# A macaron block on one core: the scheduler's durations replaced by measured ones, a slot's registers loaded once, router logits taken from the projection's product

## The chip, the core and the metric

The kernel runs on one core of a Trainium2 chip. The metric is device time in microseconds (us) of one launch. The engines have short names: PE (TensorE; PEld is its loading of weights), DVE (VectorE), ACT (ScalarE), POOL (GpSimd) and SP (SyncE, which here only issues DMAs and loads the registers that they need).

## What is computed

The input is 8 sequences of 256 tokens of 128 values (2048 tokens, 16 tiles of 128), all in float32. Six steps update it in place:

```
x = x + 0.5 * moe(layernorm(x))              # layer 0
x = x + attention(layernorm(x))              # 16 heads of 8
x = x + 0.5 * moe(layernorm(x))              # layer 1, the same weights
x = x + 0.5 * channel_mix(layernorm(x))
x = x + gated_long_convolution(layernorm(x)) # FFT of 512, filter made by a small network
x = x + 0.5 * channel_mix(layernorm(x))

def moe(s):                                  # 8 experts, each token goes to 2
    h = rmsnorm(s @ W_in.T, in_norm_w)
    logits = h @ Wr.T
    idx = top_2(logits + expert_bias);  gates = softmax(logits[idx])
    out = sum over the 2 experts e of
          gates[e] * rmsnorm((silu(h @ Wg[e].T) * (h @ Wu[e].T)) @ Wd[e].T, enorm_w[e])
    return rmsnorm(out, out_norm_w) @ W_out.T
```

## The kernel before

**Dispatch.** Both expert layers go through the tokens in four groups of four tiles (`dispatch`). A group is transposed by PE (`flip`), multiplied with the input projection (`product`, L587: four matmuls of 128x128 into one PSUM bank) and with the router's weights, which are already folded behind the projection (`logits`, L591: four matmuls with 8 columns into a second bank). DVE chooses the two experts of each token (`choice`), matmuls with a triangle of ones count the tokens of each expert (`ranks`), and POOL sends every token's row twice into a table in DRAM, `hs`, sorted by expert, with eight indirect DMAs (`scatter`, L721).

**Tables and slots.** `table` turns the counts into a list of 39 slots of 128 rows. There are two tables per layer: the one after half of the tokens gives the first 9 slots (`NFULL`), whose rows are certain by then, and the one after all of them gives the other 30. A slot (`slot`) belongs to one expert. SP makes three transfers for it: the rows (`hst`, 64.5 KB, L897), the gate and up weights (`w`, 512 KB, L889) and the down weights with the norm's weight (`wd`, 320 KB, L893). The address of each depends on the table, so SP first loads a register from it: one `values_load` for each of the three transfers (L888, L892, L896). Then PE transposes the rows (L907), does four gate and four up matmuls (L920, L924) and four down matmuls (L976); ACT and DVE do the activation between them and the norm behind them, and POOL sends the result to a second table `y2` with one indirect DMA (L1000). There are 4 buffers for `w`, 4 for `wd`, 5 for `hst`. `combine` reads `y2` back and adds to x. Then come attention (`attend`, L1192 scores and L1258 averages), the second expert layer in the same way, and the channel mixes and the convolution.

**The order.** Nothing is issued in the order of the source. Every piece of work is recorded with `plan.add`: the engines that may do it, the cost in us on each, and what it reads and writes. `Plan.best` then lists all pieces in up to 20 rounds: a forward pass (`order`) places pieces by rank on the engine that is free first and hands out buffers and PSUM banks, a backward pass (`reverse`) makes new ranks from the result, and the round with the shortest planned end is kept. That order is then issued, so each engine, SP's queue too, is an in-order list fixed when the kernel is built. The costs are formulas such as

```
def mm_(n, cols):
    return n * (0.012 + 0.00175 * cols)
def dma(nbytes, run, **k):
    return plan.add({"SP": 0.08}, lambda e: run(), size=nbytes, **k)
```

and a DMA is planned to land 2 us after its bytes passed at 250 GB/s, one transfer behind the other (`FLIGHT`, `RATE`).

Of the kernel before, what the change touches and what calls it, by code (L numbers as in the profile page):

```python
# [41 lines left out]


def mm_(n, cols):
    return n * (0.012 + 0.00175 * cols)


def dve_(cols):
    return 0.15 + cols / 960


def act_(cols, more=0.0):
# [25 lines left out]
class Plan:  # L78
# [8 lines left out]
    def add(self, engines, run, r=(), w=(), p=(), lag=0.0, table=None, size=0, boost=0.0):  # L87
        o = Op()
        o.engines, o.run, o.lag, o.table, o.size, o.boost = engines, run, lag, table, size, boost
        o.n, o.after, o.bufs = len(self.ops), [], []  # L90
        for x in (*r, *w, *p):
            if isinstance(x, Buf) and x not in o.bufs:
                o.bufs.append(x)
                self.bufs[x] = self.bufs.get(x, 0) + 1
        wait = set()
        for x, sides in [(x, (0, 1)) for x in r] + [(x, (0, 1, 2)) for x in w] + [(x, (0, 2)) for x in p]:
            s = self.state.setdefault(x, ([], [], []))
            for side in sides:
                wait.update(s[side])
        for x in r:  # L100
            self.state[x][2].append(o)
        for x in w:
            self.state[x] = ([o], [], [])
        for x in p:
            self.state[x][1].append(o)
        o.wait = wait
        o.flight = lag + (self.FLIGHT + size / self.RATE if size else 0.0)
        for b in wait:
            b.after.append(o)
        self.ops.append(o)  # L110
        return o
# [164 lines left out]
    "k4": ([P, 1024], 7),  # L276
    "k2": ([P, 516], 12),
    "k1": ([P, 256], 6),
    "hst": ([P, ROW], 5),
    "yrow": ([P, ROW], 3),  # L280
    "d": ([P, D], 5),
# [6 lines left out]
def macaron_kernel(ctx: ExitStack, tc: tile.TileContext, a: dict, out: bass.AP):  # L288
# [18 lines left out]
        return plan.add({"POOL": cost}, lambda e: run(), **k)  # L307

    def pe(cost, run, **k):
        return plan.add({"PE": cost}, lambda e: run(), **k)  # L310

    def dma(nbytes, run, **k):
        return plan.add({"SP": 0.08}, lambda e: run(), size=nbytes, **k)

    def bc_last(ap, n):
        return ap.unsqueeze(len(ap.shape)).to_broadcast([*ap.shape, n])
# [1 line left out]
    def sm():  # L318
        return Buf("sm")
# [18 lines left out]
    def X(t, n=1):  # L338
        return [("x", i) for i in range(t, t + n)]
# [157 lines left out]
    def normed_t(n, t0, wide=False):  # L497

        st = spread(n, t0)
        mr = sm()  # L500

        def scales():
            s = st.v(3 * n, "p (k t) -> p k t", k=3)
            nc.vector.tensor_scalar(mr.v(n), s[:, 0], 1.0 / D, LN_EPS, ALU.mult, ALU.add)
            nc.vector.tensor_scalar(s[:, 1], s[:, 1], 0.5, None, ALU.mult)

        dve(2 * TINY, scales, r=[], w=[st, mr])
        power(mr, n)
# [12 lines left out]
        for i in range(n):  # L521
            plan.add(
                {"POOL": 0.79, "DVE": 0.28},
                lambda e, i=i: one(e, i),
                r=[st, mr, *X(t0 + i)],
                p=[xn],
            )
        pt = Buf("bank")
        pe(0.1 * n, lambda: flip(lambda t: xn.ap[:, ts(t, D)], n, pt), r=[xn, "ident"], w=[pt])
# [19 lines left out]
        return xt  # L549
# [20 lines left out]
    def dispatch(f, t0, n, half):  # L570
        L = layer[f]
        tag = f"{f}_{t0}"
        pt, ph, pl, xt = Buf("bank"), Buf("bank"), Buf("bank"), Buf("k2")
        pe(0.1 * n, lambda: flip(lambda t: xs[:, t0 + t, :], n, pt), r=["ident", *X(t0, n)], w=[pt])
        act(act_(n * P), lambda: nc.scalar.copy(xt.v(n * P), pt.v(n * P)), r=[pt], w=[xt])
        st = spread(n, t0)
        z = sm()
# [4 lines left out]
            w=[z],  # L582
        )

        def product():
            for t in range(n):
                nc.tensor.matmul(ph.ap[:, ts(t, D)], xt.ap[:, ts(t, P)], win_r[:, 0:D], start=True, stop=True)  # L587

        def logits():
            for t in range(n):  # L590
                nc.tensor.matmul(pl.ap[:, ts(t, E)], xt.ap[:, ts(t, P)], win_r[:, D : D + E], start=True, stop=True)  # L591

        h, ll = Buf("k2"), sm()
        pe(mm_(n, D), product, r=[xt, "win_r"], w=[ph])
        pe(n * 0.07, logits, r=[xt, "win_r"], w=[pl])
        plan.add(
            {"ACT": act_(n * D), "DVE": dve_(n * D)},
            lambda e: nc.scalar.copy(h.v(n * D), ph.v(n * D))
            if e == "ACT"
            else nc.vector.tensor_copy(h.v(n * D), ph.v(n * D)),  # L600
            r=[ph],
            w=[h],
        )
        dve(TINY, lambda: nc.vector.tensor_copy(ll.v(n * E), pl.v(n * E)), r=[pl], w=[ll])
        sq, ss = Buf("k2"), sm()

        def square(t):
# [76 lines left out]
                r, ident, before.unsqueeze(1).to_broadcast([P, n + 1, E]), start=False, stop=True  # L684
            )

        pe(0.07 * (n + 2), ranks, r=[mask, "tri", "ones", "ident", prev], w=[pr])

        def place():
            v = nc.vector  # L690
# [188 lines left out]
    def slot(f, t, silu):  # L879
# [4 lines left out]
        hst, w, wd = Buf("hst"), Buf("w"), Buf("wd")  # L884
        need = [("hs", f, 0)] if early else [("hs", f, 0), ("hs", f, 1)]

        def weights():
            e = nc.values_load(tab[t : t + 1, 1:2], engines=[SP], min_val=0, max_val=E - 1)  # L888
            nc.sync.dma_start(w.ap, a["wall"][bass.ds(e, 1), :, 0 : 2 * DFF].rearrange("o p f -> p (o f)"))  # L889

        def weights_down():
            e = nc.values_load(tab[t : t + 1, 1:2], engines=[SP], min_val=0, max_val=E - 1)  # L892
            nc.sync.dma_start(wd.ap, a["wall"][bass.ds(e, 1), :, 2 * DFF : WALL].rearrange("o p f -> p (o f)"))  # L893

        def rows():
            row = nc.values_load(tab[t : t + 1, 0:1], engines=[SP], min_val=1, max_val=HS_ROWS - P)  # L896
            ins = nc.sync.dma_start(hst.ap, L["hs"][bass.ds(row, P), :])  # L897
            if early:
                alone(ins, [f"hsr{f}_0"], [f"hs{f}_1"])
                for name in L["sent"]:  # L900
                    tc.add_manual_dep(ins.ins, name, behind_data, reason="rows of the first half")

        dma(P * ROW * 4, rows, r=[("tab", f, stage), *need], w=[hst])
        dma(P * 2 * DFF * 4, weights, r=[("tab", f, stage)], w=[w])
        dma(P * (DFF + D) * 4, weights_down, r=[("tab", f, stage)], w=[wd])
        pt, ht = Buf("bank"), Buf("d")
        pe(0.12, lambda: nc.tensor.transpose(pt.v(P), hst.ap[:, 0:D], ident), r=[hst, "ident"], w=[pt])  # L907
# [7 lines left out]
        )  # L915
        pair, sg, hg = Buf("pair"), Buf("k2"), Buf("k2")

        def gate():
            for k in range(NFC):
                nc.tensor.matmul(pair.ap[:, 0, ts(k, P)], w.ap[:, ts(k, P)], ht.ap, start=True, stop=True)  # L920

        def up():
            for k in range(NFC):
                nc.tensor.matmul(  # L924
                    pair.ap[:, 1, ts(k, P)], w.ap[:, DFF + k * P : DFF + k * P + P], ht.ap, start=True, stop=True
                )

        pe(mm_(4, P), gate, r=[w, ht], p=[pair], w=[("g", f, t)])
        pe(mm_(4, P), up, r=[w, ht], p=[pair], w=[("u", f, t)])
        if silu:  # L930
            act(
                act_(DFF),
# [91 lines left out]
    def combine(f, t0, n, half):  # L1024
# [61 lines left out]
        pe(0.1 * n, lambda: flip(lambda t: acc.ap[:, ts(t, D)], n, pt), r=[acc, "ident"], w=[pt])  # L1086
# [82 lines left out]
    def attend(seqs, lead):  # L1169
# [24 lines left out]
        def set_(parts):  # L1194
# [10 lines left out]
                    pair.v2 = pair.ap.rearrange("p j (i k) -> p j i k", i=2)  # L1205
                product(parts)

            pe(mm_(2, S), run, r=r, w=w)

        def top(s, js, pair):  # L1210
            m = ms[s % NM][:, :, js[0] : js[0] + 2, HD].rearrange("p i j -> p j i")
# [7 lines left out]
        def turn_top(s):  # L1219
# [10 lines left out]
            pe(0.2, run, r=[("m", s % NM), ("m", s % NM, 0), ("m", s % NM, 2), "ident"], w=[pt])  # L1230
# [50 lines left out]
        def finish(b):  # L1281
            o = osb[b]
            cc, ct = Buf("k1"), Buf("k1")
            for i in range(2):
# [13 lines left out]
                pe(0.4, turn, r=[o, "ident"], w=[pt])  # L1298
                dve(0.5, scale, r=[pt], w=[rc], p=[cc])
            pc, pp = Buf("bank"), Buf("bank")  # L1300
            pe(0.2, lambda: flip(lambda i: cc.ap[:, ts(i, P)], 2, pc), r=[cc, "ident"], w=[pc])
            act(act_(S), lambda: nc.scalar.copy(ct.ap, pc.v(S)), r=[pc], w=[ct])

            def out_heads():
# [386 lines left out]
    with tc.manual_schedule(engines=None):  # L1691
        for o, e, takes, _, _ in todo:
            for b in takes:
                if b.kind in WIDE:
                    i = place[b][0]
                    b.ap = banks[:, i : i + 2] if b.kind == "pair" else banks[:, i]
                    continue
                shape, _ = KINDS[b.kind]
                b.ap = work.tile(shape, F32, tag=f"{b.kind}{place[b]}", name=f"{b.kind}_{o.n}")
            o.run(e)  # L1700

# [98 lines left out]
```

## Time and profile before

| | us |
|---|---|
| median of 6 runs | 678.08 |
| lowest and highest | 673.17 and 683.37 |
| the profiled execution, its own time | 679.43 |
| its span, first to last instruction | 677.7 |
| busy: PE, weight loads, DVE, ACT, POOL | 553.7, 463.1, 372.3, 258.0, 241.8 |
| mean granted clock of PE | 0.911 |
| bytes moved by DMA | 95.41 MB, 141 GB/s over the span |

The page gives busy time of each engine, then the span in 40 slices of about 17 us, where a digit is the busy share in tenths. SP's instructions are not counted as busy: they are seen in the timeline and in the views of single source lines. "q" behind an engine's name is its sequencer. In the chain that ended last, "issue" is time in which the engine waited for nothing that the profile shows. By the trace, layer 0's slots are transposed between 62 and 241 us (the last fifteen beside attention), layer 1's first nine between 374 and 448 us and its other thirty between 464 and 568 us.

### The profile page before, as it was taken

The page shows a single profiled execution, that of the slowest core. Times are in us where ns is not written, and L with a number is a line of the kernel's source. Part 1 is how long each engine was busy: PE and PEld are TensorE (multiplying, and loading weights), DVE is VectorE, ACT ScalarE, POOL GpSimd, SP SyncE. Part 2 cuts the span into 40 slices and gives each one's busy share as a digit, 9 for nine tenths or more (in the row PEclk, how much of TensorE's full clock was granted, in tenths as well). Part 3 has the DMA queues.
Part 4 walks back from the last instruction along what each step waited for, and adds up shares of the span by engine and source line. Part 5 has one row for each costly group of instructions (what it writes and reads, how often), then busy time and mean ns, then how long its engine had stood idle before and what let it go on. Part 6 is the DMA issues. An engine that isn't in the chain of part 4 may idle for free.

```text
span 677.7 us, 14362 instructions
## 1 busy us (share of the span) xinstructions
PE 553.7 (82%) x4609; PEld 463.1 (68%) x4609; DVE 372.3 (55%) x1252; ACT 258.0 (38%) x664; POOL 241.8 (36%) x407
## 2 busy tenths in 40 slices
PE   7514888888867999888988998757888887699996
PEld 7513778888756776655655667756788886578885
DVE  4635344335846668776775864642332334778762
ACT  4421233234613546744643572312222333443022
POOL 2674755223631122343040005541332325654320
PEclk9555899899979999899996999776998999599999
DMA  5147688878766603012011513557788886200002
GB/s 131 39 117 218 188 238 279 265 230 244 253 161 182 192 17 80 1 41 65 24 56 37 194 32 114 164 193 235 240 288 278 267 256 184 63 1 1 0 1 62
DMA packets 61386, 95.41 MB, mean 141 GB/s; under 512 B 9659, under 2 KB 38498, under 8 KB 61312
## 3 DMA queue, kind: packets, MB, share of 16 engines
q1 hardware_dynamic: 56480, 84.98, 41.6%
q0 software_dynamic: 4832, 9.53, 4.0%
q8 instruction: 36, 0.59, 0.4%
q14 instruction: 38, 0.31, 0.2%
HBM read 81.68 MB, written 13.71 MB: 141 GB/s over the span
## 4 chain that ended last, share of the span: by engine, by line
PE 60%; DMA 9%; issue 9%; DVE 9%; SPq 6%; ACT 3%; POOL 2%; another core or an unknown queue 2%; DVEq 0%; ACTq 0%; POOLq 0%
PE banks L920 9%; PE banks L1192 8%; PE banks L976 8%; PE banks L924 8%; DMA hst<-hs 6%; PE banks L1258 5%; PE banks L495 2%; ACT k L1243 2%; PE banks L1588 2%; PE banks L1623 2%; PE banks L1353 2%; PE banks L1363 2%; PE banks L907 2%; DVE m L1214 1%
## 5 line engine op out<-in xcount | busy, mean ns | idle before, releaser
L1000 POOL DMA_INDIRECT y<-yrow,hst x78 | 76.8, 985 | 195.9 <-DVE yrow L993 142.7
L976 PE MATMUL banks<-wd,k 128*128 128x128 f32 x624 | 90.0, 290 | 23.1 <-DMA wd<-in_wall_dram 10.7
L488 POOL TENSOR_TENSOR sm<-sm,mhalf 128x4 f32<-128x4 f32 (+2 forms) x52 | 50.9, 985 | 152.2 <-DVE sm L615 77.6
L976 PEld LDWEIGHTS banks<-wd,k 128*128 128x128 f32 x624 | 79.8, 200 | 30.0 <-issue 9.1
L920 PE MATMUL banks<-d,w 128*128 128x128 f32 x624 | 90.8, 292 | 11.7 <-ACT d L910 4.5
L920 PEld LDWEIGHTS banks<-d,w 128*128 128x128 f32 x624 | 81.8, 205 | 17.4 <-ACT d L910 7.1
L1214 DVE TENSOR_REDUCE m<-banks 128x4 f32<-128x1024 f32 x64 | 77.5, 1222 | 27.5 <-PE banks L1192 23.0
L924 PE MATMUL banks<-d,w 128*128 128x128 f32 x624 | 89.2, 289 | 3.6 <-issue 3.3
L924 PEld LDWEIGHTS banks<-d,w 128*128 128x128 f32 x624 | 82.2, 205 | 5.5 <-issue 5.4
L1243 ACT ACTIVATE k<-banks 128x1024 f32<-128x1024 f32 x64 | 64.3, 1023 | 48.8 <-PE banks L1192 43.5
L721 POOL DMA_INDIRECT hs<-row,sm x64 | 62.1, 970 | 36.2 <-issue 24.8
L1192 PE MATMUL banks<-k,q 32*128 32x256 f32 x512 | 72.6, 420 | 1.6 <-issue 1.5
L941 DVE TENSOR_TENSOR k<-banks,k 128x512 f32<-128x512 f32 x53 | 36.6, 691 | 65.7 <-PE banks L924 35.0
L1192 PE MATMUL banks<-k,k 32*128 32x256 f32 x512 | 69.3, 409 | 1.6 <-DVE m L1214 1.0
L933 ACT ACTIVATE k<-banks 128x512 f32<-128x512 f32 x53 | 31.5, 597 | 79.0 <-PE banks L920 50.1
L1192 PEld LDWEIGHTS banks<-k,q 32*128 32x128 f32 x512 | 45.8, 197 | 15.1 <-issue 9.1
L987 ACT ACTIVATE d<-banks 128x128 f32<-128x128 f32 x78 | 21.5, 276 | 79.7 <-PE banks L976 63.4
L1192 PEld LDWEIGHTS banks<-k,k 32*128 32x128 f32 x512 | 45.6, 193 | 5.7 <-issue 1.8
L993 DVE TENSOR_TENSOR yrow<-banks,wd 128x128 f32<-128x128 f32 x78 | 22.2, 288 | 39.9 <-ACT d L987 31.2
L1258 PE MATMUL banks<-k,v 128*32 128x256 f32 x512 | 35.4, 395 | 7.7 <-ACT k L1243 4.1
L907 PE MATMUL banks<-ident,hst 128*128 128x128 f32 x78 | 22.7, 310 | 19.6 <-DMA hst<-hs 17.7
L912 DVE TENSOR_SCALAR d<-banks,inw 128x128 f32<-128x128 f32 x44 | 14.8, 348 | 33.9 <-PE banks L907 31.7
(229 smaller groups left out, 901.3 us busy)
## 6 DMA issues: line engine op xcount, KB each, us to landing
w<-in_wall_dram SPq DMA_DIRECT2D x78, 512.0 KB
wd<-in_wall_dram SPq DMA_DIRECT2D x78, 320.0 KB
hst<-hs SPq DMA_DIRECT2D x78, 64.5 KB
row<-y SPq DMA_DIRECT2D x16, 129.0 KB
row<-y SPq DMA_DIRECT2D x8, 258.0 KB
y<-yrow,hst POOLq DMA_INDIRECT x78
xs<-in_x_dram SPq DMA_DIRECT2D x4, 256.0 KB
hs<-row,sm POOLq DMA_INDIRECT x64
```

What stands on the lines that cost most here:

```text
L488: lambda: nc.gpsimd.tensor_tensor(buf.v(n), buf.v(n), mhalf.to_broadcast([P, n]), ALU.pow),
L721: ins = nc.gpsimd.indirect_dma_start(out=L["hs"], out_offset=bass.IndirectOffsetOnAxis(ap=posi.ap[:, 2 * n + 2 * t + k : 2 * n + 2 * t + k ...
L907: pe(0.12, lambda: nc.tensor.transpose(pt.v(P), hst.ap[:, 0:D], ident), r=[hst, "ident"], w=[pt])
L920: nc.tensor.matmul(pair.ap[:, 0, ts(k, P)], w.ap[:, ts(k, P)], ht.ap, start=True, stop=True)
L924: nc.tensor.matmul(pair.ap[:, 1, ts(k, P)], w.ap[:, DFF + k * P : DFF + k * P + P], ht.ap, start=True, stop=True)
L941: lambda: nc.vector.tensor_mul(hg.v(DFF), pair.ap[:, 1], sg.v(DFF)),
L976: nc.tensor.matmul(py.v(D), hg.ap[:, ts(k, P)], wd.ap[:, ts(k, D)], start=(k == 0), stop=(k == NFC - 1),)
L1000: ins = nc.gpsimd.indirect_dma_start(out=L["y2"], out_offset=bass.IndirectOffsetOnAxis(ap=hst.ap[:, D : D + 1].bitcast(I32), axis=0), in_= ...
L1192: nc.tensor.matmul(o, l, m, start=True, stop=True)
L1214: lambda: nc.vector.tensor_reduce(m, pair.v2, AX.X, ALU.max, negate=True),
L1243: lambda: nc.scalar.activation(es.v(1024, "p (j i k) -> p j i k", j=2, i=2), pair.v2, AF.Exp, scale=SCALE),
L1258: nc.tensor.matmul(po.ap[32 * j : 32 * j + 32, 0:S], vs[b % NQ][:, i, 4 * g + j, :], ess[s, j // 2 * 2].v(1024, "p (j i k) -> p j i k", j= ...
```

## The change

Three things are changed. Numbers of lines in this section's text are those of the kernel before.

1. The planner's costs are new. A group of matmuls costs 0.07 us and at least 0.224 us each, a group of transposes 0.1 us and 0.11 us each (`turn_`), DVE work 0.01 us more, and what PE makes is ready 0.12 us after its end. A DMA takes 0.42 us of SP instead of 0.08. The pieces that a piece waits for are sorted, so that the plan is the same in every build. Every piece can so get another place, another engine and another buffer.
2. A slot loads its row and its expert number into registers of SP in one piece, `registers`, planned at 0.55 us, and the three transfers use these. At most ten slots hold registers at a time. The gate and up matmuls of a slot become one piece of eight matmuls.
3. The router's logits are eight more columns of the projection's product: four matmuls of 136 columns, two in each bank of a pair, in place of four of 128 and four of 8. What copies the product and the logits out reads the pair.

```diff
 def mm_(n, cols):
-    return n * (0.012 + 0.00175 * cols)
+    return 0.07 + n * max(0.224, 0.00176 * cols)
+
+
+def turn_(n):
+    return 0.1 + 0.11 * n
 
 
 def dve_(cols):
-    return 0.15 + cols / 960
+    return 0.16 + cols / 960
...
+        wait = sorted(wait, key=lambda b: b.n)
         o.wait = wait
...
     "k1": ([P, 256], 6),
+    "regs": (None, 10),
...
     def pe(cost, run, **k):
-        return plan.add({"PE": cost}, lambda e: run(), **k)
-
-    def dma(nbytes, run, **k):
-        return plan.add({"SP": 0.08}, lambda e: run(), size=nbytes, **k)
+        return plan.add({"PE": cost}, lambda e: run(), lag=0.12, **k)
+
+    def dma(nbytes, run, issue=0.42, **k):
+        return plan.add({"SP": issue}, lambda e: run(), size=nbytes, **k)
...
-        pt, ph, pl, xt = Buf("bank"), Buf("bank"), Buf("bank"), Buf("k2")
-        pe(0.1 * n, lambda: flip(lambda t: xs[:, t0 + t, :], n, pt), r=["ident", *X(t0, n)], w=[pt])
+        pt, ph, xt = Buf("bank"), Buf("pair"), Buf("k2")
+        pe(turn_(n), lambda: flip(lambda t: xs[:, t0 + t, :], n, pt), r=["ident", *X(t0, n)], w=[pt])
...
         def product():
             for t in range(n):
-                nc.tensor.matmul(ph.ap[:, ts(t, D)], xt.ap[:, ts(t, P)], win_r[:, 0:D], start=True, stop=True)
-
-        def logits():
-            for t in range(n):
-                nc.tensor.matmul(pl.ap[:, ts(t, E)], xt.ap[:, ts(t, P)], win_r[:, D : D + E], start=True, stop=True)
...
+                nc.tensor.matmul(parts()[:, t // m, t % m, :], xt.ap[:, ts(t, P)], win_r, start=True, stop=True)
+
+        pe(mm_(n, wide), product, r=[xt, "win_r"], w=[ph])
...
-        pe(0.07 * (n + 2), ranks, r=[mask, "tri", "ones", "ident", prev], w=[pr])
+        pe(mm_(n + 2, 1), ranks, r=[mask, "tri", "ones", "ident", prev], w=[pr])
...
-        def weights():
-            e = nc.values_load(tab[t : t + 1, 1:2], engines=[SP], min_val=0, max_val=E - 1)
-            nc.sync.dma_start(w.ap, a["wall"][bass.ds(e, 1), :, 0 : 2 * DFF].rearrange("o p f -> p (o f)"))
...
+        values = {}
+
+        def registers():
+            _, (row, e) = nc.values_load_multi_w_load_instructions(
+                tab[t : t + 1, 0:2], engines=[SP], min_val=0, max_val=HS_ROWS - P
+            )
+            values["row"], values["e"] = row, nc.s_assert_within(e, 0, E - 1)
 
         def rows():
-            row = nc.values_load(tab[t : t + 1, 0:1], engines=[SP], min_val=1, max_val=HS_ROWS - P)
-            ins = nc.sync.dma_start(hst.ap, L["hs"][bass.ds(row, P), :])
+            ins = nc.sync.dma_start(hst.ap, L["hs"][bass.ds(values["row"], P), :])
...
-        dma(P * ROW * 4, rows, r=[("tab", f, stage), *need], w=[hst])
-        dma(P * 2 * DFF * 4, weights, r=[("tab", f, stage)], w=[w])
-        dma(P * (DFF + D) * 4, weights_down, r=[("tab", f, stage)], w=[wd])
+        def part(to, lo, hi):
+            nc.sync.dma_start(to.ap, a["wall"][bass.ds(values["e"], 1), :, lo:hi].rearrange("o p f -> p (o f)"))
+
+        regs = Buf("regs")
+        plan.add({"SP": 0.55}, lambda e: registers(), r=[("tab", f, stage)], w=[regs])
+        dma(P * ROW * 4, rows, r=[regs, *need], w=[hst])
+        dma(P * 2 * DFF * 4, lambda: part(w, 0, 2 * DFF), r=[regs], w=[w])
+        dma(P * (DFF + D) * 4, lambda: part(wd, 2 * DFF, WALL), r=[regs], w=[wd])
...
-        pe(mm_(4, P), gate, r=[w, ht], p=[pair], w=[("g", f, t)])
-        pe(mm_(4, P), up, r=[w, ht], p=[pair], w=[("u", f, t)])
+        pe(mm_(8, P), gate_up, r=[w, ht], p=[pair], w=[("g", f, t), ("u", f, t)])
...
-            pe(mm_(2, S), run, r=r, w=w)
+            pe(mm_(2, S) + 0.1, run, r=r, w=w)
```

More of the change, by code (lines that the diff above doesn't have):

```diff
@@ L528, in normed_t @@
         pt = Buf("bank")
-        pe(0.1 * n, lambda: flip(lambda t: xn.ap[:, ts(t, D)], n, pt), r=[xn, "ident"], w=[pt])
+        pe(turn_(n), lambda: flip(lambda t: xn.ap[:, ts(t, D)], n, pt), r=[xn, "ident"], w=[pt])
         xt = Buf("k2")
@@ L583, in dispatch, with parts, keep @@
         )
+        h, ll = Buf("k2"), sm()
+        m = n // 2
+        wide = D + E
+        def parts():
+            return ph.ap[:, :, 0 : m * wide].rearrange("p i (j d) -> p i j d", j=m)
         def product():
             for t in range(n):
-                nc.tensor.matmul(ph.ap[:, ts(t, D)], xt.ap[:, ts(t, P)], win_r[:, 0:D], start=True, stop=True)
-        def logits():
-            for t in range(n):
[L591 to L600, printed above, removed]
+                nc.tensor.matmul(parts()[:, t // m, t % m, :], xt.ap[:, ts(t, P)], win_r, start=True, stop=True)
+        pe(mm_(n, wide), product, r=[xt, "win_r"], w=[ph])
+        def keep(e):
+            dst = h.v(n * D, "p (i j d) -> p i j d", i=2, j=m)
+            src = parts()[:, :, :, 0:D]
+            nc.scalar.copy(dst, src) if e == "ACT" else nc.vector.tensor_copy(dst, src)
+        plan.add({"ACT": act_(n * D), "DVE": dve_(n * D)}, keep, r=[ph], w=[h])
+        dve(
+            TINY,
+            lambda: nc.vector.tensor_copy(
+                ll.v(n * E, "p (i j e) -> p i j e", i=2, j=m), parts()[:, :, :, D:wide]
+            ),
             r=[ph],
-            w=[h],
+            w=[ll],
         )
-        dve(TINY, lambda: nc.vector.tensor_copy(ll.v(n * E), pl.v(n * E)), r=[pl], w=[ll])
         sq, ss = Buf("k2"), sm()
@@ L885, in slot @@
         need = [("hs", f, 0)] if early else [("hs", f, 0), ("hs", f, 1)]
-        def weights():
[L888 to L893, printed above, removed]
+        values = {}
[4 more added lines that the diff above has]
+            values["row"], values["e"] = row, nc.s_assert_within(e, 0, E - 1)
         def rows():
-            row = nc.values_load(tab[t : t + 1, 0:1], engines=[SP], min_val=1, max_val=HS_ROWS - P)
-            ins = nc.sync.dma_start(hst.ap, L["hs"][bass.ds(row, P), :])
+            ins = nc.sync.dma_start(hst.ap, L["hs"][bass.ds(values["row"], P), :])
             if early:
@@ L901, in rows @@
                     tc.add_manual_dep(ins.ins, name, behind_data, reason="rows of the first half")
-        dma(P * ROW * 4, rows, r=[("tab", f, stage), *need], w=[hst])
-        dma(P * 2 * DFF * 4, weights, r=[("tab", f, stage)], w=[w])
-        dma(P * (DFF + D) * 4, weights_down, r=[("tab", f, stage)], w=[wd])
+        def part(to, lo, hi):
[5 more added lines that the diff above has]
+        dma(P * (DFF + D) * 4, lambda: part(wd, 2 * DFF, WALL), r=[regs], w=[wd])
         pt, ht = Buf("bank"), Buf("d")
-        pe(0.12, lambda: nc.tensor.transpose(pt.v(P), hst.ap[:, 0:D], ident), r=[hst, "ident"], w=[pt])
+        pe(turn_(1), lambda: nc.tensor.transpose(pt.v(P), hst.ap[:, 0:D], ident), r=[hst, "ident"], w=[pt])
         plan.add(
@@ L916, in slot, with gate_up @@
         pair, sg, hg = Buf("pair"), Buf("k2"), Buf("k2")
[L918 to L926, printed above, removed]
-        pe(mm_(4, P), gate, r=[w, ht], p=[pair], w=[("g", f, t)])
-        pe(mm_(4, P), up, r=[w, ht], p=[pair], w=[("u", f, t)])
+        def gate_up():
+            for half in range(2):
+                for k in range(NFC):
+                    nc.tensor.matmul(
+                        pair.ap[:, half, ts(k, P)],
+                        w.ap[:, half * DFF + k * P : half * DFF + k * P + P],
+                        ht.ap,
+                        start=True,
+                        stop=True,
+                    )
+        pe(mm_(8, P), gate_up, r=[w, ht], p=[pair], w=[("g", f, t), ("u", f, t)])
         if silu:
@@ L1085, in combine @@
         pt, at = Buf("bank"), Buf("k2")
-        pe(0.1 * n, lambda: flip(lambda t: acc.ap[:, ts(t, D)], n, pt), r=[acc, "ident"], w=[pt])
+        pe(turn_(n), lambda: flip(lambda t: acc.ap[:, ts(t, D)], n, pt), r=[acc, "ident"], w=[pt])
         act(act_(n * P), lambda: nc.scalar.copy(at.v(n * P), pt.v(n * P)), r=[pt], w=[at])
@@ L1228, in run @@
                     )
-            pe(0.2, run, r=[("m", s % NM), ("m", s % NM, 0), ("m", s % NM, 2), "ident"], w=[pt])
+            pe(turn_(2), run, r=[("m", s % NM), ("m", s % NM, 0), ("m", s % NM, 2), "ident"], w=[pt])
             dve(
@@ L1296, in scale @@
                     )
-                pe(0.4, turn, r=[o, "ident"], w=[pt])
+                pe(turn_(4), turn, r=[o, "ident"], w=[pt])
                 dve(0.5, scale, r=[pt], w=[rc], p=[cc])
             pc, pp = Buf("bank"), Buf("bank")
-            pe(0.2, lambda: flip(lambda i: cc.ap[:, ts(i, P)], 2, pc), r=[cc, "ident"], w=[pc])
+            pe(turn_(2), lambda: flip(lambda i: cc.ap[:, ts(i, P)], 2, pc), r=[cc, "ident"], w=[pc])
             act(act_(S), lambda: nc.scalar.copy(ct.ap, pc.v(S)), r=[pc], w=[ct])
@@ L1698, in macaron_kernel @@
                 shape, _ = KINDS[b.kind]
+                if shape is None:
+                    continue
                 b.ap = work.tile(shape, F32, tag=f"{b.kind}{place[b]}", name=f"{b.kind}_{o.n}")
```

## The prediction

> **What bounds the kernel now.** First I read the page: busy time and the slices.
>
> ```profile
> PE 553.7 (82%) x4609; PEld 463.1 (68%) x4609; DVE 372.3 (55%) x1252; ACT 258.0 (38%) x664; POOL 241.8 (36%) x407
> DMA  5147688878766603012011513557788886200002
> ```
>
> TensorE (PE) is the busiest engine, but 82% averages unlike stages. The DMA row has two humps: layer 0's expert slots (about 42 to 240 us) and layer 1's (425 to 570). So I took the slots by themselves: the transposes at L907, one per slot, in two stretches that hold little else (columns: length, PE busy and count, weight loads, clock, DMA share, GB/s).
>
> ```profile
> 84.00:160.00 76.00, 5.36 (x20) 2.69 (x20) 0.98 0.81 250
> 462.00:563.00 101.00, 8.05 (x28) 4.10 (x28) 0.95 0.82 256
> ```
>
> A slot takes 76/20 = 3.80 us in layer 0 and 101/28 = 3.61 us in layer 1. What should it take? PE: gate, up and down take 0.89 us each at full clock (chain of waits, first line below) and the transpose at most 0.33, so 2.8 to 3.0 us. DMA: a slot moves 512 + 320 + 64.5 KB in and 64.5 KB out, 0.984 MB; the second line (all engines; the last three numbers are clock, DMA share, GB/s) gives 274/0.87 = 315 GB/s at full share, so 3.12 us.
>
> ```profile
> 103.17 0.89 PE banks L924 x8
> 500.00:540.00 40.00, 34.64 (x269) 32.33 (x270) 12.82 (x30) 10.98 (x33) 11.63 (x24) 0.96 0.87 274
> ```
>
> Neither reaches 3.6. The SyncE (SP) queue does: its timeline in layer 0, one transfer after another.
>
> ```profile
> 94.69 0.33 SPq L889 DMA_DIRECT2D w<-in_wall_dram  x1
> 95.86 0.33 SPq L893 DMA_DIRECT2D wd<-in_wall_dram  x1
> 97.03 0.33 SPq L897 DMA_DIRECT2D hst<-hs  x1
> 98.18 0.47 SPq L889 DMA_DIRECT2D w<-in_wall_dram  x1
> 99.33 0.33 SPq L897 DMA_DIRECT2D hst<-hs  x1
> 100.52 0.33 SPq L893 DMA_DIRECT2D wd<-in_wall_dram  x1
> ```
>
> Five steps in 5.83 us: 1.166 us per transfer, 3.50 per slot, with hardly a wait between. SP is the limit of both stretches, though no busy row shows it. The views of the lines that issue say what fills 1.166 us (duration minimum/median/maximum, ns):
>
> ```profile
> L888 SPq TENSOR_LOAD <-tab x78: 77/274/711, 40.1 to 558.0; - x78
> L888 SPq FUSED_REGOPS  x78: 2/152/697, 40.6 to 558.4; - x78
> L888 SPq SEQ_ASSERT  x78: 3/18/402, 40.9 to 558.6; - x78
> L889 SPq FUSED_REGOPS  x78: 5/37/685, 40.9 to 558.6; - x78
> L889 SPq MOVE w<-in_wall_dram x78: 3/29/707, 41.5 to 558.8; - x78
> L889 SPq DMA_DIRECT2D w<-in_wall_dram x78: 11/333/694, 42.9 to 558.8; - x78
> ```
>
> The six medians sum to 0.843 us; with a semaphore instruction (median 0.017) 0.860. The remaining 0.306 over seven instructions is 0.044 us between two.
>
> **The change, part by part.** *Registers once.* The built program of the changed kernel has, per slot, one group of a load, two FUSED_REGOPS, three SEQ_ASSERTs and one register operation, and per transfer a FUSED_REGOPS, a semaphore instruction, a MOVE and the DMA. The group: 0.274 + 2 x 0.152 + 3 x 0.018 + 7 x 0.044 = 0.94 us, and the register operation itself, which no row shows: between 0.018 and 0.152; being one plain operation I take it like the assert, so 0.96. If the second FUSED_REGOPS no longer waits for the load it costs 0.037, and the group 0.84; high end 1.09. A transfer: 0.037 + 0.017 + 0.029 + 0.333 + 4 x 0.044 = 0.59. A slot: 0.96 + 3 x 0.59 = 2.73 us (2.6 to 2.9) against 3.50. Then DMA, at 3.12, is next late. A queue in order with four buffers of each weight does not run DMA at 100%: the best 6 us stretches of the windows are at 0.90 to 0.93. I take 3.30 us in layer 1 (share 0.945) and 3.45 in layer 0, where the filter's matmuls share PE and windows fall to 0.63. Ends: 3.12 (DMA always full) and today's 3.61 and 3.80 (nothing).
> Layer 1: 28 x 0.31 = 8.7 us (0 to 13.7). Layer 0: 20 x 0.35 = 7.0 us (0 to 13.6).
> Layer 0's last 15 slots run beside attention, where PE bounds, except in two holes (columns as in the second line two fences up):
>
> ```profile
> 192.00:198.00 6.00, 1.06 (x10) 0.87 (x8) 1.30 (x5) 0.87 (x4) 2.95 (x6) 0.82 0.46 109
> 210.00:216.00 6.00, 2.76 (x23) 2.52 (x23) 1.27 (x5) 1.29 (x6) 1.23 (x3) 1.00 0.36 85
> 437.00:462.00 25.00, 13.37 (x81) 12.45 (x81) 8.65 (x31) 3.51 (x12) 11.46 (x22) 0.77 0.64 226
> ```
>
> PE idles 4.9 + 3.2 = 8.2 us in the first two, while SP works off register loads and head copies; I take half, 4 us (0 to 8).
>
> A page of the Trainium skill speaks against all this. "DMA: Bandwidth & Descriptors" (section "Issuing engines are not separate DMA queues") says that the sequencer time to start a DMA is usually small beside the transfer; by that rule these 20 us would be nothing and the total about 670. The row decides here: 1.166 us of issue against 64.5 KB / 315 GB/s = 0.2 us for hst and 1.7 us for w. The same page (section "Specifications") puts a core's HBM limit near 358 GB/s; as an estimate, 0.984 MB then takes 2.75 us, PE would bound, and the slots would gain some 40 us.
>
> *Logits from the product.* Gone are 32 matmuls of 8 columns in 8 dispatches.
>
> ```profile
> L591 PE MATMUL banks<-win_r,k 128*128 128x8 f32 x64 | 9.4, 273 | 0.0
> 9.59 1.51 PE banks L591 x8
> ```
>
> 9.4 us of PE in all; the 8 columns more per product give back 8/128 of L587's 12.4 us, 0.8. On the path are the first group (1.5 us in the chain) and layer 1's four, half of 9.4 in a stage where PE is 85 to 95% busy: 4.2. Less 0.8 x 0.7: 5 us (1.5 to 8.6). The pair of banks replaces two banks; the copies keep their sizes.
>
> *The new order.* New costs (SP 0.42 and 0.55 instead of 0.08, matmul 0.07 + 0.224 each, 0.12 lag) move every queue. Three places decide.
> Start: nine groups (8.6 us) now stand before the first hst in place of nine loads of 0.274 + 0.152 + 0.018 + 3 x 0.044 = 0.58 (5.2), and the 512 KB dft table too. Between 41 and 56 us, while POOL issues layer 0's scatters, SP's instructions stretch to 0.7 us, so the first hst could be 4 us later; but DVE now makes table 0 ahead of the next dispatch's 15 choice instructions (15 x 0.22 = 3.3 us earlier). I take 0 (+4 to -4).
> Behind the fifth hst SP then waits for the second table; queued there are the weights of slots 4 to 8 and the next four hst, for which PE waits. That table was ready at 66 us, and the first weight buffer comes free about then: nothing, +3 if it slips.
> Gate and up are one step of eight matmuls, no longer parted by other work; ACT still starts after gate's four: 0.
> Layer 1's last dispatch (third line of the fence above): PE idles 25 - 13.4 = 11.6 us, until SP at last issues the first late hst:
>
> ```profile
> 459.67 1.89 SPq L897 DMA_DIRECT2D hst<-hs  x2
> 461.22 3.54 DMA hst<-hs
> ```
>
> The scatters it needs were issued by 445.5, so SP was some 12 us behind them, in register loads, weights and two 512 KB tables (now later). In the new order hst comes after five register groups and six weights (5 x 0.96 + 6 x 0.59 = 8.3 us), which overlap the scatters. But the early slots that fill PE here today stand mostly before the last rank matmuls. I take 3 us gained (10 gained to 11 lost: four slots of 2.85 us no longer hidden).
> Attention and the tail from 572 us keep their instructions and are PE-bound: 0 (+3 to -3).
>
> **Sum.** 8.7 + 7.0 + 4 + 5 + 0 + 3 = 27.7 us less than the profiled execution's 679.4 (span 677.7 and 1.7 around it): 651.7. That execution lies 1.3 us above the median of the runs, so **650 us**, and with every piece at its best end 617, at its worst 698. They hardly fall together; a third of the way to each end is 639 to 666.
>
> **Rivals.** *The slots stay as they are* (about 672): buffers, not SP, set the pace; four w buffers are released at PE's pace, and SP only waits longer. For it: semaphore waits of up to 3.6 us on w in 60 to 120 us. Against: the even 1.17 us steps. Price: only logits and a little remain, 5 to 8 us. This includes the case that the change doesn't do what it says.
> *The hole in layer 1 opens* (about 664): early slots delay the last dispatch by 11 us and nothing covers its scatters; 14 us of the gain go.
> *Slower: rows behind weights* (about 690). All of SP's transfers share one hardware queue. hst now lands 3.5 to 4.0 us after issue; SP freed of its loads puts one more slot's weights ahead of it (0.852 MB / 315 GB/s = 2.7 us), and the new order issues hst often in pairs, behind two w. PE already waits for hst 18 times, 17.7 us. If half of some 24 pairs show 1.4 us more, PE loses 17 us and the slot gains vanish: 678 - 5 + 17 = 690. It decides once hst takes over 6 us to land and the five hst buffers don't hide it.
>
> **How the numbers follow.** Forecast 0.52, opened hole 0.15, unchanged slots 0.13, rows behind weights 0.20. About 1% is what a measurement of this kernel can tell. Faster takes the first two and a quarter of the third: 0.70; same 0.10; slower 0.20. The range, 630 to 688, reaches into the slow case and leaves a tenth at each side; the forecast's own is 639 to 666.
>
> **What would show it.** Right: SP steps within a slot near 0.6 us after one group near 1 us, slots at 3.2 to 3.5 us in both stretches, DMA share above 0.9 there, no 128x8 matmuls, PE idle shorter around the last table. Wrong: slots still at 3.6 with SP waiting on PE's semaphores; hst landing after 6 us; or the first late slot starting more than 30 us after the last ranks.

## The result, and the profile after

The changed kernel takes 693.94 us (median of 20 runs, 691.48 to 699.09) against 677.85 us (46 runs): a ratio of 1.028, 95% interval 1.0253 to 1.0304. It is slower, and the forecast of 650 us was wrong in sign.

The page of after, three rows:

```profile
PE 540.4 (78%) x4545; PEld 453.4 (65%) x4545; DVE 374.3 (54%) x1252; ACT 256.6 (37%) x658; POOL 246.5 (36%) x413
DMA  5137578888686202021116134166788685100002
L924 PE MATMUL banks<-ident,hst 128*128 128x128 f32 x78 | 22.5, 313 | 54.4 <-DMA hst<-hs 42.4
```

PE has less work but waits more: 42.4 us for the rows of a slot alone (17.7 before). Two slot stretches, by the transposes (now L924; columns as in the prediction), and then four windows of all engines:

```profile
84.00:160.00 76.00, 5.31 (x20) 2.85 (x20) 0.93 0.83 266
470.00:571.00 101.00, 7.49 (x26) 3.78 (x26) 0.94 0.78 252
```

```profile
500.00:540.00 40.00, 31.43 (x236) 29.46 (x235) 11.33 (x27) 9.59 (x30) 11.55 (x22) 0.92 0.83 263
192.00:198.00 6.00, 3.81 (x40) 2.51 (x39) 4.61 (x7) 1.01 (x5) 2.09 (x4) 1.00 0.94 313
210.00:216.00 6.00, 5.95 (x64) 4.53 (x62) 2.85 (x5) 2.08 (x6) 1.05 (x2) 1.00 0.82 219
441.00:467.00 26.00, 0.73 (x7) 0.53 (x5) 6.26 (x42) 2.10 (x6) 12.61 (x24) 0.58 0.49 171
```

In layer 1, 26 slots fit where 28 did. PE is busier at 192 and 210, but in the hole around layer 1's last table it now does 0.73 us of work in 26. The register group on SP (durations minimum/median/maximum, ns), and a piece of SP's timeline:

```profile
L903 SPq FUSED_REGOPS  x156: 3/152/700, 29.0 to 542.3; - x156
L903 SPq SEQ_ASSERT  x156: 3/18/1385, 29.2 to 542.5; - x156
L903 SPq TENSOR_LOAD <-tab x78: 3/485/1376, 28.2 to 541.5; - x78
```

```profile
516.72 0.33 SPq L909 DMA_DIRECT2D hst<-hs  x1
517.28 0.33 SPq L916 DMA_DIRECT2D w<-in_wall_dram  x1
517.85 0.33 SPq L909 DMA_DIRECT2D hst<-hs  x1
520.87 0.33 SPq L916 DMA_DIRECT2D wd<-in_wall_dram  x1
```

The steps are 0.57 us, near the 0.59 that was worked out; the 3.02 us at the end hold a register group and a wait. What SP waits for in the late slots (us in total, times, longest), before from 480 to 572 us and after from 486 to 580:

```profile
SPq L897 <- DMA y<-yrow,hst: 1.7, 3, 0.9
```

```profile
SPq L909 <- DMA y<-yrow,hst: 14.6, 9, 3.0
SPq L916 <- DVE yrow L1010: 5.2, 6, 1.3
...
SPq L916 <- PE banks L938: 3.7, 5, 1.5
SPq L916 <- PE banks L924: 2.3, 3, 1.1
```

Freed of its loads, SP stands at a rows' transfer until the y scatter of an earlier slot gives a place of hst back, with weights queued behind. PE waits for the table and the rows in the hole (after, 437 to 468 us) like this:

```profile
PE banks L924 <- DMA hst<-hs: 25.6, 1, 25.6
```

Where the 16.2 us went, from the starts of the transposes and the ends of the down products in both traces (slots counted in PE's order; us):

| point | before | after | difference | in this stage |
|---|---|---|---|---|
| first slot starts | 61.8 | 69.4 | +7.6 | +7.6 |
| 24th slot ends | 164.2 | 163.4 | -0.8 | -8.4 |
| layer 1's first slot | 374.5 | 366.7 | -7.8 | -7.0 |
| first late slot | 464.2 | 467.3 | +3.1 | +10.9 |
| last slot ends | 573.6 | 582.2 | +8.6 | +5.5 |
| span | 677.7 | 693.9 | +16.2 | +7.6 |

The tail (before, then a piece and the whole of after's) by windows of all engines:

```profile
573.60:677.70 104.10, 90.33 (x520) 74.28 (x519) 70.27 (x271) 32.86 (x84) 39.24 (x45) 0.93 0.08 21
```

```profile
606.00:612.00 6.00, 6.00 (x16) 3.93 (x17) 4.24 (x26) 1.23 (x2) 3.92 (x7) 0.50 0.01 3
582.20:693.90 111.70, 93.39 (x520) 76.54 (x520) 70.69 (x270) 34.62 (x88) 44.63 (x51) 0.89 0.08 22
```

PE idles 18.3 us there instead of 13.8 and needs 3.1 us more for the same 520 products, at a mean granted clock of 0.89 instead of 0.93.

### The profile page after: what moved, and what is told of

It reads as the page before. It is cut to its first block, busy times and chain, and to the rows that moved or that the text cites. A ratio compares the mean times of both kernels' runs of the same rounds, so it can differ in the third digit from the quotient of the medians.

```text
span 693.9 us, 14017 instructions
## 1 busy us (share of the span) xinstructions
PE 540.4 (78%) x4545; PEld 453.4 (65%) x4545; DVE 374.3 (54%) x1252; ACT 256.6 (37%) x658; POOL 246.5 (36%) x413
## 5 line engine op out<-in xcount | busy, mean ns | idle before, releaser
L938 PE MATMUL banks<-d,w 128*128 128x128 f32 x1248 | 167.8, 294 | 8.5 <-issue 3.1
L938 PEld LDWEIGHTS banks<-d,w 128*128 128x128 f32 x1248 | 160.0, 209 | 14.2 <-issue 4.9
L993 PE MATMUL banks<-wd,k 128*128 128x128 f32 x624 | 84.7, 281 | 3.9 <-DMA wd<-in_wall_dram 1.8
L993 PEld LDWEIGHTS banks<-wd,k 128*128 128x128 f32 x624 | 76.9, 195 | 8.3 <-DVE yrow L1010 2.1
L1209 PE MATMUL banks<-k,q 32*128 32x256 f32 x512 | 68.3, 402 | 4.3 <-issue 3.6
L1209 PE MATMUL banks<-k,k 32*128 32x256 f32 x512 | 66.1, 400 | 3.1 <-ACT k L1260 3.1
L924 PE MATMUL banks<-ident,hst 128*128 128x128 f32 x78 | 22.5, 313 | 54.4 <-DMA hst<-hs 42.4
L929 DVE TENSOR_SCALAR d<-banks,inw 128x128 f32<-128x128 f32 x52 | 17.7, 349 | 79.5 <-PE banks L924 75.2
L924 PEld LDWEIGHTS banks<-ident,hst 128*128 128x128 f32 x78 | 11.4, 149 | 60.6 <-DMA hst<-hs 45.0
L1209 PEld LDWEIGHTS banks<-k,k 32*128 32x128 f32 x512 | 42.8, 186 | 5.2 <-ACT k L1260 3.8
L501 PE MATMUL banks<-ident,k 128*128 128x128 f32 x112 | 21.9, 308 | 13.3 <-DVE k L1084 8.8
```

Of the source, the lines that this page charges most:

```text
L924: pe(turn_(1), lambda: nc.tensor.transpose(pt.v(P), hst.ap[:, 0:D], ident), r=[hst, "ident"], w=[pt])
L938: nc.tensor.matmul(pair.ap[:, half, ts(k, P)], w.ap[:, half * DFF + k * P : half * DFF + k * P + P], ht.ap, start=True, stop=True,)
L993: nc.tensor.matmul(py.v(D), hg.ap[:, ts(k, P)], wd.ap[:, ts(k, D)], start=(k == 0), stop=(k == NFC - 1),)
L1209: nc.tensor.matmul(o, l, m, start=True, stop=True)
```

## The experiments

Each ratio is against before on the same chip, with its 95% interval. e1 to e4, e5 to e8, e9 to e12 and e17 with e18 went on four chips on which before takes 681 to 684 us, e13 to e16 on a fifth, where it takes 645.92. The chip can move a ratio: e15 and e18 are one kernel, at 0.9531 and 0.9778. So a difference of two ratios from different chips is less sure than their intervals say. Theory 1 is that the new order, not the edits, makes the loss; theory 2 that the register group does; theory 3 that buffers (the numbers of places in KINDS) set the slots' pace.

**One part at a time.** e1_old_order_regs:

```diff
 def weights():  # the same in weights_down and rows
-    e = nc.values_load(tab[t : t + 1, 1:2], ...)
+    e = registers()[1]   # loads both values if not yet loaded
```

> The order of before on every engine, with a slot's two registers loaded once, in front of whichever of its three transfers SP issues first; nothing else is changed. Theory 1 (the new order is what costs): the register edit is good by itself, SP's work per slot falls from 3.5 us to about 3.0 (1.2 for the load group as the trace after shows it, 3 x 0.6), so 48 slots of the two SP-bound stretches give 0.2 to 0.4 us each: 660 to 670 us. Theory 2 (the register group harms, since it stands in front of the rows' transfer): 685 to 695. Theory 3 (buffers set the pace of the slots in any order): 675 to 680.

Measured: 681.88 us, 1.0016 (0.9982 to 1.0049): no gain. e2_new_order_three_loads puts the loads back in after:

```diff
 def part(to, lo, hi):  # and rows
-    nc.sync.dma_start(to.ap, a["wall"][bass.ds(values["e"], 1), ...
+    e = nc.values_load(tab[t : t + 1, 1:2], ...)
+    nc.sync.dma_start(to.ap, a["wall"][bass.ds(e, 1), ...
```

> The order of after on every engine, with the register of each transfer loaded by itself again, as in before. Theory 1 (order): the registers loaded once are worth something in this order too, so undoing them costs 5 to 15 us: 699 to 709 us. Theory 2 (the register group harms): 675 to 685. Theory 3 (buffers): 690 to 698, no difference.

Measured: 700.12 us, 1.0291 (1.0222 to 1.0361), the ratio of after. The time lies in theory 1's 699 to 709, but only because before takes 681.34 us on this chip. So the register edit by itself shows no gain in either order, neither that of theory 1 nor the harm of theory 2. Why, SP's waits in layer 0 (84 to 160 us) tell, before and then e1:

```profile
SPq L897 <- DMA y<-yrow,hst: 3.0, 2, 2.7
```

```profile
SPq L907 <- DMA y<-yrow,hst: 9.9, 10, 1.7
SPq L903 <- DVE yrow L1003: 2.2, 4, 1.1
```

9.9 us in 10 waits instead of 3.0 in 2: the time saved at the loads is spent waiting for the places of hst. e3_before_new_durations changes the durations alone:

```diff
-    return n * (0.012 + 0.00175 * cols)
+    return 0.07 + n * max(0.224, 0.00176 * cols)
-    return plan.add({"SP": 0.08}, ...
+    return plan.add({"SP": 0.6}, ...
 ...
```

> Before, with only the planner's durations changed to those of after (a transfer on SP at 0.6 us, so that a slot's three cost SP what after's four steps do); three register loads and the separate logit matmuls stay. Theory 1 (order): 695 to 710 us, the loss of after and more. Theories 2 and 3, and a loss that came with the fused logits: 672 to 683.

Measured: 684.59 us, 1.0073 (1.003 to 1.0116): slower, but a quarter of the loss; 695 to 710 was wrong. e4_after_old_durations is the reverse edit in after:

```diff
-    return 0.07 + n * max(0.224, 0.00176 * cols)
+    return n * (0.012 + 0.00175 * cols)
-    plan.add({"SP": 0.55}, lambda e: registers(), ...
+    plan.add({"SP": 0.08}, lambda e: registers(), ...
 ...
```

> After, with the planner's durations of before (the register load at 0.08 us like a transfer); registers loaded once, logits from the product and gate and up as one step stay. Theory 1 (order): 655 to 672 us, a gain. Theory 2 (register group) or a loss from the fused logits: 688 to 697.

Measured: 697.55 us, 1.0244 (1.0179 to 1.031). The loss stays without the new durations, which theory 1 did not expect. This would point to the edits' structure; e7_old_order_three_edits holds the order of before instead:

```diff
+nc.tensor.matmul(parts((ph, pl)[t // m])[:, t % m, :], xt.ap[:, ts(t, P)], win_r, ...)
 ...
-def up():   # its four matmuls now stand in gate()
-pe(mm_(4, P), up, r=[w, ht], ...
+pe(mm_(4, P), lambda: None, r=[w, ht], ...
 # and registers() as in e1
```

> The order of before with all three edits of the structure: registers once, gate and up as one run of eight matmuls, and the logits from the product of 136 columns, here two tiles in each of the two banks that before has for product and logits, so that one copy becomes two of half the size; one of eight dispatches keeps its separate logits, since its second bank is in use between. Theory 1 (order): the structure by itself does no harm: 670 to 681 us. If the edits' structure is what costs (fused gate and up delays ACT's Silu, or wide products hold banks): 685 to 698.

Measured: 681.02 us, 0.9963 (0.9927 to 0.9999). The structure does no harm where the order is kept. So by exclusion it is in e4 too the order found around the new steps.

**The order as a draw.** e8_control_tiny:

```diff
-TINY = 0.17
+TINY = 0.18
```

> Before with one planning cost changed by 0.01 us: the small VectorE operations count as 0.18 instead of 0.17. Nothing in the program's work changes, only the order that the planner finds. Theory 1 in its strong form (any new order is a draw, and before's is a lucky one): 685 to 705 us. If the loss of after belongs to its durations or its structure: 674 to 683.

Measured: 697.72 us, 1.0228 (1.0171 to 1.0286), from one planning cost moved by 0.01 us and no other edit. Its page, beside that of before in the prediction:

```profile
PE 556.4 (80%) x4609; PEld 465.8 (67%) x4609; DVE 376.5 (54%) x1258; ACT 256.8 (37%) x658; POOL 243.4 (35%) x407
DMA  5155678888766302012161023378888874000002
```

The same work and instructions on PE; the last slot ends 7.0 us later (580.6) and the tail is 11.3 us longer (115.4). e16_control_slack:

```diff
-    LAG, SLACK, SWITCH, FLIGHT, RATE = 0.15, 0.1, 1.3, 2.0, 0.25e6
+    LAG, SLACK, SWITCH, FLIGHT, RATE = 0.15, 0.11, 1.3, 2.0, 0.25e6
```

> Before with the planner's SLACK at 0.11 instead of 0.10 and nothing else, a second order of the same work beside the eighth experiment. Theory 1 in its strong form: off before by over 1%, 686 to 700 us (the planner's own total is 609 us against 600 for before and 621 for the eighth experiment). If such small changes are harmless and the eighth experiment was an outlier: 676 to 684.

Measured: 649.11 us, 1.0057 (1.0018 to 1.0095): a second draw, worse than before by less than expected. e10_new_slack0 draws another order for after:

```diff
-    LAG, SLACK, SWITCH, FLIGHT, RATE = 0.15, 0.1, 1.3, 2.0, 0.25e6
+    LAG, SLACK, SWITCH, FLIGHT, RATE = 0.15, 0.0, 1.3, 2.0, 0.25e6
```

> After with the planner's SLACK at 0 instead of 0.1: an operation may go first only where none can start earlier. All durations and the program's work are those of after; the planner's own total for this order is 631 us instead of 651. Theory 1 (the loss of after is the order that was drawn): another order of the same kernel differs by over 1%, and if the planner's own totals tell orders of one set of durations apart, it is faster, 670 to 685 us. If the loss belongs to what after does in any order: 688 to 698.

Measured: 684.77 us, 1.0042 (1.0009 to 1.0075). With the same durations and edits, some 2% of after's loss is gone with the order. PE's waits around the last table (425 to 470 us) show one place of it:

```profile
PE banks L938 <- DVE d L929: 8.2, 2, 7.8
PE banks L924 <- DMA hst<-hs: 4.9, 1, 4.9
```

The wait for the first late rows is 4.9 us instead of 25.6, and the tail 102.4 us instead of 111.7.

The planner's own totals, which stand in the expectations of e16 and e10, go with the times here: 600, 609 and 621 us for before, e16 and e8, at 1, 1.0057 and 1.0228; 651 and 631 for after and e10, at 1.028 and 1.0042. Five orders are few, and totals made with different durations can't be compared (600 and 631 are nearly the same time).

**Places.** e5_old_order_regs_places (order of before, registers once, larger numbers at emission):

```diff
+more, turn = {"hst": 10, "w": 6, "wd": 6, "yrow": 6}, {}
 ...
-b.ap = work.tile(shape, F32, tag=f"{b.kind}{place[b]}", ...)
+b.ap = work.tile(shape, F32, tag=f"{b.kind}{at}", ...)  # at: given out in turn
```

> The kernel of the first experiment (order of before, registers once) with the rows' tile in 10 places instead of 5, both weight tiles in 6 instead of 4 and yrow in 6 instead of 3, given out in turn when the program is written; the planner still counts the old numbers, so that the order on every engine stays. Theory 3 (buffers took over from SP as the pace: SP waits for the y scatter that frees a rows' tile 18 times there): the waits vanish, slots come near 3.2 us, 48 of them give 12 to 20 us: 660 to 670 us. If PE's order and its waits on other engines set the pace: 677 to 683, no difference.

Measured: 664.43 us, 0.9718 (0.9662 to 0.9774). e9_old_order_places is the same edit in before, with its three loads:

> Before (three register loads per slot) with the larger numbers of places of the fifth experiment and its order unchanged. If SP's issue of 3.5 us per slot was a limit of its own, as the prediction read it, the places alone bring little: 675 to 681 us, and only both together bring the 17 us of the fifth experiment. If SP was never a limit and buffers alone set the pace: 662 to 668.

Measured: 671.55 us, 0.987 (0.9805 to 0.9935): between the two answers. Alone, registers give nothing, places 1.3%, both 2.8%, on three chips. SP's timeline of e9 in the late slots shows what limits places alone there:

```profile
503.55 0.34 SPq L889 DMA_DIRECT2D w<-in_wall_dram  x1
504.76 1.50 SPq L897 DMA_DIRECT2D hst<-hs  x2
507.07 0.33 SPq L889 DMA_DIRECT2D w<-in_wall_dram  x1
508.26 0.32 SPq L893 DMA_DIRECT2D wd<-in_wall_dram  x1
```

Four steps in 4.71 us, 1.18 each: SP issues without a pause, and from 462 to 563 us the slots' transfers wait 0.4 us in all. The window 500 to 540 of e9, then of e5:

```profile
500.00:540.00 40.00, 32.85 (x268) 30.41 (x268) 13.01 (x29) 11.30 (x34) 10.43 (x20) 1.00 0.86 268
```

```profile
500.00:540.00 40.00, 35.39 (x293) 33.28 (x294) 13.77 (x33) 12.38 (x38) 12.08 (x24) 1.00 0.93 302
```

With both, DMA is at a share of 0.93 (0.87 before, 0.86 in e9). e12_old_order_regs_hst10 is e5 with one kind:

```diff
-more, turn = {"hst": 10, "w": 6, "wd": 6, "yrow": 6}, {}
+more, turn = {"hst": 10}, {}
```

> The first experiment (order of before, registers once) with only the rows' tile in 10 places; weights and yrow as in before. If the rows' tile, freed by the y scatter of five slots earlier, is the buffer that sets the pace (SP waits for it 10 and 8 times in the two stretches, for the others under 7 times): 664 to 670 us. If the weights' four places are the next limit at once: 673 to 681.

Measured: 676.09 us, 0.99 (0.9857 to 0.9943): below e1, and the second answer's time. By ratios from three chips hst is a good third of what places give beside registers; the places of weights and yrow are the rest. e6_new_order_places is after with the edit of e5:

> After with the same larger numbers of places and its own order on every engine. Theory 3 (buffers): layer 1's late slots are back at 3.3 us or less, 26 x 0.45 = 12 us, and the first slots gain too: 675 to 685 us. Theory 1 (order: the rows' transfers stand where the order puts them): a few us, 688 to 693.

Measured: 680.04 us, 0.9972 (0.9939 to 1.0005), some 3% under after. The same two windows as above, by L924:

```profile
84.00:160.00 76.00, 5.39 (x21) 2.94 (x21) 0.98 0.87 291
470.00:571.00 101.00, 7.45 (x28) 4.08 (x28) 0.97 0.81 273
```

From the first late transpose to the last down product the 30 late slots take (us): before 109.4, after 114.9, e1 108.5, e9 106.9, e5 104.6, e6 102.7. From the first slot's start to the 24th's end: before 102.4, e1 100.1, e9 96.1, e5 96.9. So the registers show beside places in the late slots (2.3 us), not in the first ones.

**Together.** e11_old_order_three_edits_places is e7 with the places of e5; e14_old_order_regs_logits_places is e11 with gate and up as two steps:

```diff
-pe(mm_(4, P), lambda: None, r=[w, ht], ...
+pe(mm_(4, P), up, r=[w, ht], ...
```

> The seventh experiment (order of before, all three edits of the structure) with the larger numbers of places. Theory 1 with 3: the gains add, 17 us from registers with places and 2 to 4 from logits and gate and up: 658 to 665 us, faster than before and after. If wide products or fused gate and up take something back once buffers are free: 666 to 675.

> The eleventh experiment without its second edit: order of before, registers once, logits from the product, more places; gate and up stay two steps. If gate and up as one run takes something back: 658 to 663 us. If not, and the difference between the fifth and the eleventh experiment was scatter: 664 to 669.

Measured: e11 669.41 us, 0.9829 (0.977 to 0.9887); e14 631.43 us, 0.9762 (0.9705 to 0.9819), on the chip of 645.92. The intervals overlap: whether gate and up as one run takes something back isn't settled. e11 ran beside e9 on one chip and has all of e5's edits and two more, yet it stands only 0.4% below e9, with intervals that overlap: what registers are worth once there are places, 1.5% by e5 on another chip, isn't settled either. e15_new_slack0_places is e10 with the places; e18_slack0_places_beside is the same kernel on another chip, and e17_after_beside is after, unchanged, beside it:

> The tenth experiment (after with SLACK 0) with the larger numbers of places. If places and order are separate terms: 12 to 16 us less than the tenth, 669 to 673 us, below before. If the order at SLACK 0 already asks for fewer places: 678 to 684.

> After, unchanged, beside the next kernel and before on one chip. On a chip where before takes about 680 us: 697 to 702 (its ratio 1.028 again). On one where before takes about 646: 658 to 666 if the ratio holds, and then e13's 652 means that the early register groups cost some 9 us; 650 to 654 if the chip moves the ratio, and then e13's edit is worth nothing.

> The kernel of e15, unchanged, beside after and before on one chip. If its gain belongs to the kernel: 0.953 of before wherever it runs, 647 to 652 where before takes 680. If part of it belongs to that chip (the first bound was 669 to 673 from adding the two terms): 665 to 675 where before takes 680.

Measured: e15 615.13 us, 0.9531 (0.9479 to 0.9583); e18 667.34 us, 0.9778 (0.973 to 0.9826); e17 700.29 us, 1.023 (1.0161 to 1.0299). All of the change, in an order drawn anew and with more places, beats before on both chips, and after on the one where after ran; 2 to 3% of e15's gain belongs to its chip. e13_new_order_lazy_regs loads the registers in after where e1 does:

```diff
-plan.add({"SP": 0.55}, lambda e: registers(), ...
+plan.add({"SP": 0.55}, lambda e: None, ...   # loaded in front of the first transfer
```

> After with its own order on all engines, but a slot's two registers are loaded in front of the first of its three transfers and not at the step that the planner placed for them. If those early groups in front of the first rows' transfer are what delays the first slot (69.4 us against 61.8), the first slot starts near 65 us and the time falls by 3 to 6 us: 691 to 695 beside a before of 681. If the delay comes from the rest of the order: no change, 696 to 700.

Measured: 652.25 us, 1.0127 (1.0052 to 1.0203). On that chip after itself was not run, and e15 and e18 show that it moves ratios by 2%; so what the early register groups cost stays open. The traces of e2 and after, one order without and with the groups, put it at 5.1 us for the first slot (64.3 against 69.4), and the 24th slot ends at 162.9 and 163.4: the slots in between win it back.

## Why the prediction was wrong

**The step that failed first: "Then DMA, at 3.12, is next late."** The steps of a transfer came out near the sum, 0.57 us for 0.59. The group was mis-sized, 0.485 + 2 x 0.152 + 3 x 0.018 + 0.035 + 7 x 0.044 = 1.19 us instead of 0.96, as a load of two values takes 0.485 us and not the 0.274 of one; a slot is then 2.96 us on SP, not 2.73, still below 3.12. But right behind SP's limit, and above DMA's 3.12, stood a third one that the sum left out: a place of hst is held from issue until the y scatter has landed, and with five of them, and four of each weight, the late slots of e1 still take 108.5 / 30 = 3.62 us. As an estimate from e1's trace, from the sixth late slot on a place is held 13.9 us to the scatter's end and some 3 us more to its landing; 17 us over five places are 3.4 us a slot, and 3.42 is the pace at which SP issues rows there. So the terms of 8.7 and 7.0 us came to nothing in the total (e1, 1.0016), and the first rival ("buffers, not SP, set the pace") had the mechanism, though it named the w buffers and not hst.

With more places the terms came in part, and not for SP's sake alone. e5's trace (the slowest of its four runs, 669.49 us) gains 5.5 us in the first 24 slots and 4.8 in the 30 late ones, where the sum had 7.0 and 8.7; e9 with three loads gains 6.3 and 2.5 at the same points. SP is a limit of its own in e9's late slots, where it issues without a pause; in layer 0, which the prediction read as bound by SP too, the runs don't show it. The trace of before has 3.0 us of waits on hst in layer 0; a wait that is short because another limit hides it was read as no limit.

The page "DMA: Bandwidth & Descriptors" of the Trainium skill (section "Issuing engines are not separate DMA queues"), which the prediction set aside by its row, gave the outcome of e1: 1.0016. The row is right that 1.17 us of issue isn't small beside the transfers, but it didn't decide; with more places the two loads that are saved are worth between 0.4% (e11 against e9) and 1.5% (e5 against e9).

**The second step: "Three places decide."** By the table above: the start +7.6 (taken as 0, at most 4), the stage with layer 1's last dispatch +10.9 (taken as -3, bound 11), the tail +7.6 (taken as 0, at most 3), attention with its two holes, and layer 1's first dispatches, -7.0 (taken as -4 and a part of the logits' 5). The hole is the second rival's: the early slots end at 441.7 us, before the last scatters are issued (451.9), and nothing covers them. From the first slot to the 24th layer 0 gained 8.4 us, near the 7.0 of the sum, but that is luck: it makes up for the start's 7.6, and e2 with three loads ends its 24th slot at 162.9 as well, having started at 64.3. Layer 1's slots lost 5.5 us where 8.7 were to be gained.

The term was not mis-sized only, it was of the wrong kind. I costed the order as shifts at known places; e8 shows that an order of the same work, found after a change of 0.01 us, is 2.3% slower. Five other orders of nearly the same work (e3, e4, e8, e10, e16) lie 0.4 to 2.4% above before, none below. That after's loss is its draw is shown by e7 (edits without a new order, 0.9963) and e10 (another order, 1.0042). How much a draw costs hangs on the places too: after's own order with more of them takes what before does (e6, 0.9972), though the order of before with the same places and edits is still faster (e11, 0.9829, on another chip).

**What held.** Logits from the product: no 128x8 matmuls. Their worth isn't shown: e7 less e1 is 0.5% (3.6 us, with gate and up as one run and one copy more per dispatch), inside 1.5 to 8.6, but the intervals overlap and the chips differ. The third rival (rows behind weights, 690) had the sign and nearly the time, by luck: PE waits 9.7 us for rows in the late slots instead of 5.3, not because they land late behind weights but because SP may not issue them, 14.6 us of waits for places in after against 1.7 before. By the packets of 516 bytes in the traces a late slot's rows have passed 3.1 us after their issue on average in after, 5.8 at most, and 2.6 in before; the rival wanted over 6.

## What to carry to other kernels

When an issue queue is the bound, work out what the next limits are with the queue taken away, and count the time that each buffer is held (issue to the last reader's landing, over the number of places) beside the engines and the DMA; undo one limit and the next may stand a few per cent below it. Measured under the old limit that time is too short: by the same estimate it is some 15 us in before's late slots, 3.0 us a slot, and grew to 17 when SP issued sooner (e1). When an order is found by a search, an edit of its costs or steps is a new draw: hold the old order at first to price the edit (e1, e7), then draw several orders, compare their planned totals with the times, and only then speak of the edit's worth.

## What the hardware showed

A TENSOR_LOAD of two values took 485 ns on SP (median of 78), one of a single value 274.

In after's tail PE is busy for 0.89 us of the 3 from 603 to 606, and its granted clock is 0.50 from 606 to 612 (window above); there the products of 512 columns (L1380) take 1061 to 1220 ns instead of 592:

```profile
L1380 PE MATMUL banks<-k,k_new x2: 1061/1140/1220, 606.0 to 607.0; 128*128 128x512 f32 x2
```

In before small products come first, at half speed too (421 to 476 ns until 591.4 us, 275 from 591.8), and the large ones (L1363) take 593 to 595 ns from the first at 592.4. The page "TensorE: Matmul & The Clock Gate" of the Trainium skill (section "What's actually happening") says that PE runs at half rate after an idle window and recovers after some 3.4 us of work; the trace agrees in the half rate, and shows some 6 us of it here.

The kernel of e15 and e18 spans 611.8 us on one chip and 664.4 on another. The engines' instructions last the same (gate and up products 287 and 289 ns on average, row scatters 971 and 969), but beside POOL's scatters ahead of the first table VectorE's small instructions follow each other differently. Windows of e18 and then e15 (third pair of columns: DVE busy and count):

```profile
34.00:58.00 24.00, 0.36 (x2) 0.36 (x2) 5.68 (x34) 4.05 (x9) 16.52 (x31) 0.50 0.31 93
```

```profile
31.00:47.00 16.00, 0.63 (x3) 0.63 (x4) 6.44 (x38) 5.58 (x11) 13.61 (x25) 0.50 0.81 268
```

On the first chip 34 instructions of 0.17 us are spread over 24 us; on the other 38 fit in 16, and the ranks that wait for them start 11 us sooner (46.4 against 57.6). The first slot is 20.7 us ahead there (51.2 against 71.9); 32.6 more come between layer 0's last slot and the first late one, where layer 1's dispatches run, and the tail gives nothing. What makes it was not tried.
